# Taking the group statistics in a pass of their own and turning the image inside the layer norm

## The chip, the cores and the metric

One Trainium2 chip, one core. The metric is the device time of the kernel in microseconds (us): the median over runs of one build. Everything is fp32.

## The reference

The kernel computes four residual blocks on one image `x` of 256 x 256 pixels and 128 channels. Ahead of each block the image goes through a group norm with 32 groups of 4 channels. Only block 0 (attention over rows) and the layer norms of block 2 are touched. Cut to what matters:

```python
def _gn(v, G=32, eps=1e-5):                       # over the whole image, per group of channels
    g = v.reshape(B_, H_, W_, G, C_ // G)
    m = jnp.mean(g, axis=(1, 2, 4), keepdims=True)
    s = jnp.var(g, axis=(1, 2, 4), keepdims=True)
    return ((g - m) / jnp.sqrt(s + eps)).reshape(v.shape)

def _L0_conv_ref(z, ...):                         # z = _gn(x)
    mu = jnp.mean(z, axis=-1, keepdims=True)      # layer norm over the 128 channels of a pixel
    var = jnp.mean(jnp.square(z - mu), axis=-1, keepdims=True)
    zn = (z - mu) * jax.lax.rsqrt(var + EPS) * ln_scale + ln_bias
    q, k, v = zn @ Wq, zn @ Wk, zn @ Wv           # 4 heads of 32
    bias = zn @ Wb                                # one number per pixel and head
    ...

x = x + _L0_conv_ref(_gn(x), ...)                 # attention
x = x + _L1_conv_ref(_gn(x), ...)                 # recurrence in a transformed domain
x = x + _L2_conv_ref(_gn(x), ...)                 # triangle product, two layer norms
x = x + _L3_conv_ref(_gn(x), ...)                 # 3 x 3 convolution
```

## The kernel before

The input lies pixel by pixel, the kernel works channel by channel: 128 channels on 128 partitions, pixels along the free dimension. `run` goes through these stages one after the other; between stages the whole image (33.5 MB) goes out to HBM and comes back.

1. **Transposing stage** (`transpose_in`, L158 to L216). 64 blocks of 1024 pixels. SP loads a block of `x`, TensorE turns it in 8 transposes of 128 x 128 into the PSUM tile `pt`, VectorE (L208) and ScalarE (L206) each copy one half of it into `xo` in SBUF, VectorE takes `BATCH_NORM_STATS2` of `xo` (L211), and GpSimd issues the DMA that writes `xo` to the HBM image `xT` (L212). In between, `spectrum` makes the transforms of the recurrence's small kernels: TensorE products `ph`, ScalarE copies `H` (L188) and `HH` (L192), and a DMA to `HD`. `attention_weights` and `bounded` prepare block 0's weights on small tiles.
2. **Group norm's mean and variance** (`group_affine`, `centering`). A short chain on single columns; it yields `lc`, a 128 x 128 matrix that applies group norm and takes off the mean over channels in one product, and its constant `cb`.
3. **Layer norm stage of block 0** (first part of `attention`). For each block of 1024 pixels: product `zc` of `lc` with `xin`, loaded from `xT`; ScalarE squares `zc` to `sq`; VectorE adds `cb` and copies `zc` to `zs`; a product of `sq` with the full matrix `omat` gives the variance of each pixel on all 128 partitions at once (`var`, 128 x 1024); ScalarE takes its logarithm and exponential (`rs`); VectorE multiplies `zs` by `rs`; GpSimd applies scale and bias. For each 2048 pixels (a piece, in what follows) the products `pbias` with 32 weight columns follow, four side by side in one PSUM bank, the copy `bi`, four small DMAs to `biasD`, and a DMA of `zn` to the HBM image `znT`.
4. Attention itself (`attend_bounded`), then the recurrence.
5. **Triangle block** (`triangle`): its first layer norm (32 pieces), the triangle products, its last layer norm with gates (32 pieces).
6. The convolution.

The order of the work on each engine is written out in the program. What is wrapped in `pin` (`keep_in_program_order`) keeps its place; a scheduler may move the rest[...]. Pools with `bufs=n` rotate through n buffers, and a writer waits until the last reader of the old content is done. Where two engines read the same PSUM tile, the built program makes the second reader wait for the first.

The triangle's first layer norm already takes its variance with 32 weight columns (`tmean`), four products side by side in one bank, so that logarithm and exponential work on 128 x 512 and not on 128 x 1024; a second product, `pr`, spreads the result over the partitions:

```python
def variance(ps, work, sq):
    var = ps.tile([P, 512], F32, name="var", tag="r", bufs=2)
    for k in range(4):
        mm(var[32 * k:32 * k + 32], m32, sq[k // 2][:, (k % 2) * 512:(k % 2 + 1) * 512])
    rs = work.tile([P, 512], F32, name="rs")
    act(rs, var, AF.Ln, bias=self.eps)
    act(rs, rs, AF.Exp, scale=-0.5)
    return rs
```

Of the kernel before, what the change touches and what calls it, by code (L numbers as in the profile page):

```python
# [30 lines left out]
class Kernel:  # L31
# [43 lines left out]
    def group_affine(self, pool, psum, stats, group, tag, whole=False, shift=None):  # L75
# [20 lines left out]
        pm = psum.tile([P, 2], F32, name=f"pm{tag}", tag="gn")  # L96
        self.mm(pm[:, 0:1], group, mv[:, 0:1])
        mg = pool.tile([P, 1], F32, name=f"mg{tag}")
        nc.vector.tensor_copy(mg, pm[:, 0:1])
        d = pool.tile([P, 1], F32, name=f"gd{tag}")  # L100
        nc.vector.tensor_sub(d, mv[:, 0:1], mg)
        v = pool.tile([P, 1], F32, name=f"gv{tag}")
        nc.vector.scalar_tensor_tensor(v, d, d, mv[:, 1:2], ALU.mult, ALU.add)
        pv = psum.tile([P, 2], F32, name=f"pv{tag}", tag="gn")
        self.mm(pv[:, 0:1], group, v)
        sd = pool.tile([P, 1], F32, name=f"sd{tag}")
        self.chain("table", self.act(sd, pv[:, 0:1], AF.Sqrt, bias=self.eps))
        ab = pool.tile([P, 2], F32, name=f"ab{tag}")
        nc.vector.reciprocal(ab[:, 0:1], sd)
        nc.vector.scalar_tensor_tensor(ab[:, 1:2], mg, -1.0, ab[:, 0:1], ALU.mult, ALU.mult)  # L110
        if whole:
            return ab, mg, sd
        return ab
# [44 lines left out]
    def transpose_in(self, xT, HD_, stats):  # L158

        nc, tc, I = self.nc, self.tc, self.i
        x = I["x"].rearrange("b h w c -> (b h w) c")
        CG = HC // 4
        with ExitStack() as c:
            sp = c.enter_context(self.pool(name="sp", bufs=1))
            io = c.enter_context(self.pool(name="p0", bufs=5))
            ps = c.enter_context(self.pool(name="p0s", bufs=3, space=PSUM))
            tu = self.load(sp, I["c_rows"], "tu")
            HH = sp.tile([46, N, HC], F32, name="HH")  # L170
            H, ka = [], []
            for n, (re, im) in enumerate((("A_real", "A_imag"), ("B_real", "B_imag"))):
                kr, ki = (I["L1_conv_" + y].rearrange("c p q -> p c q") for y in (re, im))
                k = sp.tile([3 * KS, HC, 32], F32, name=f"ka{n}")
                nc.gpsimd.memset(k, 0.0)
                for p0, q0, src in ((0, 0, kr), (0, KS, ki), (KS, 0, ki), (2 * KS, KS, kr)):
                    nc.scalar.dma_start(k[p0:p0 + KS, :, q0:q0 + KS], src)
                ka.append(k)
                H.append(sp.tile([P, N, CG], F32, name=f"H{n}"))

            def spectrum(g):

                n, g0 = divmod(2 * g, CG)
                ph = ps.tile([P, 2, N], F32, name="ph", bufs=2)
                for j in range(2):
                    for k in range(4):
                        self.mm(ph[32 * k:32 * k + 32, j], ka[n][:, CG * k + g0 + j, :], tu)
                nc.scalar.copy(H[n][:, :, g0:g0 + 2].rearrange("q u c -> q c u"), ph)  # L188
                if g0 + 2 == CG:
                    o = slice(32 * n, 32 * n + 2 * KS)  # L190
                    for k in range(4):
                        nc.scalar.copy(HH[o, :, CG * k:CG * (k + 1)], H[n][32 * k:32 * k + 2 * KS])  # L192
                    nc.sync.dma_start(HD_[n], HH[o])

            NB = NPIX // 1024
            for b in range(NB):
                xin = io.tile([P, 8, P], F32, name="xin")
                nc.sync.dma_start(xin, x[b * 1024:(b + 1) * 1024].rearrange("(p t) c -> p t c", t=8))
                xo = io.tile([P, P, 8], F32, name="xo")
                pt = ps.tile([P, 8, P], F32, name="pt")  # L200
                for t in range(8):
                    nc.tensor.transpose(pt[:, t, :], xin[:, t, :], self.ident)
                for h in range(2):
                    o, i = xo[:, :, 4 * h:4 * h + 4], pt[:, 4 * h:4 * h + 4, :].rearrange("c t p -> c p t")
                    if h:
                        nc.scalar.copy(o, i)  # L206
                    else:
                        nc.vector.tensor_copy(o, i)  # L208
                xf = xo.rearrange("c p t -> c (p t)")
                for h in range(2):  # L210
                    nc.vector.bn_stats(stats[:, 2 * b + h, :], xf[:, h * 512:(h + 1) * 512])  # L211
                nc.gpsimd.dma_start(xT[:, b * 1024:(b + 1) * 1024], xf)  # L212
                if b == NB * 7 // 8 - 1:
                    self.early_statistics(stats, "0")
                if b >= 12 and b % 3 == 0 and b < 60:
                    spectrum(b // 3 - 4)  # L216

    def attention_weights(self, wp):

        nc, tc, I = self.nc, self.tc, self.i  # L220
        with self.pool(name="awp", bufs=1, space=PSUM) as ps0:
            def load(src, name):
                t = wp.tile(list(src.shape), F32, name=name)
                nc.scalar.dma_start(t, src)
                return t
            lns, lnb = (load(I["L0_conv_ln_" + n].rearrange("(c o) -> c o", o=1), "ln" + n[0]) for n in ("scale", "bias"))
            w, wb, raws = {}, {}, {}

            for nm, f in (("q", -1.0 / math.sqrt(HD)), ("k", 1.0), ("v", 1.0), ("g", 1.0), ("b", -1.0)):
                raw = raws[nm] = load(I["L0_conv_W" + nm], "raw" + nm)  # L230
                m = raw.shape[1]
                pb = ps0.tile([P, 2], F32, name="pb" + nm, tag="gn")
                self.mm(pb[:m, 0:1], raw, lnb)
                wb[nm] = wp.tile([m, 1], F32, name="wb" + nm)
                nc.vector.tensor_scalar_mul(wb[nm], pb[:m, 0:1], 0.5 if nm == "g" else f)
                w[nm] = wp.tile([P, m], F32, name="w" + nm)
                nc.vector.tensor_scalar(w[nm], raw, lns, f, ALU.mult, ALU.mult)
            wo = {"f": load(I["L0_conv_Wo"], "wo"), "h": wp.tile([P, P], F32, name="woh")}
            nc.vector.tensor_scalar_mul(wo["h"], wo["f"], 0.5)
            self.lnb = lnb  # L240
        small = self.bounded(wp, raws, w, wb)
# [7 lines left out]
        return w, (lns, lnb), wo, small  # L249
# [21 lines left out]
    def attention(self, wp, weights, later, xT, x1T, znT, biasD, stats0, stats1, shift1):  # L271
        nc, tc, I = self.nc, self.tc, self.i
        w, (lns, lnb), wo, small = weights
        with ExitStack() as c:
            with ExitStack() as c1:
                ps0 = c1.enter_context(self.pool(name="awq", bufs=2, space=PSUM))
                ab, mg, _ = self.group_affine(wp, ps0, stats0, self.g4, "0", True)
                nc.vector.tensor_scalar_mul(shift1, mg, -1.0)
                lc, cb = self.centering(wp, ps0, ab, "0")

            bias = wp.tile([P, 2, NH, N], F32, name="bias")
            first = tuple(wp.tile([P, 1024], F32, name=n) for n in ("zn0", "xr0"))

# [9 lines left out]
            with ExitStack() as c1:  # L293
                io = c1.enter_context(self.pool(name="a1", bufs=3))
                work = c1.enter_context(self.pool(name="a1w", bufs=3))
                ps = c1.enter_context(self.pool(name="a1s", bufs=2, space=PSUM))
                V = nc.vector
                wb32 = w["32"]
                pin = lambda f: lambda *a, **k: tc.keep_in_program_order(f(*a, **k))
                mm, act, tt, ts = pin(self.mm), pin(self.act), pin(V.tensor_tensor), pin(V.tensor_scalar_add)  # L300
                copy = pin(V.tensor_copy)
                flat = lambda t: t.rearrange("p k n -> p (k n)")
                NB = NPIX // 1024
                xin, zn, zc, zs, sq = {}, {}, {}, {}, {}

                def centre(b):
                    if b >= NB:
                        return
                    if b % 2 == 0:
                        xin[b // 2] = io.tile([P, 2048], F32, name="xin")  # L310
                        nc.sync.dma_start(xin[b // 2], xT[:, b * 1024:(b + 2) * 1024])
                        zn[b // 2] = io.tile([P, 2048], F32, name="zn")
                    zc[b] = ps.tile([P, 2, 512], F32, name="zc")
                    for k in range(2):
                        s = (b % 2) * 1024 + k * 512
# [22 lines left out]
                def pair_bias(m):  # L338
                    if m < 0:
                        return  # L340
# [1119 lines left out]
```

## Time and profile before

| what | value |
|---|---|
| median of 3 runs | 5201.29 us (5197.82 to 5203.03) |
| profiled execution | 5192.49 us, of which the span of the profile is 5190.7 us |
| busy share of the span | TensorE 95%, VectorE 79%, ScalarE 69%, GpSimd 8% |
| start to first transposes | 0 to 21 us |
| transposing stage | 21 to 221 us |
| group norm's mean and variance | 221 to 225.4 us |
| layer norm stage of block 0 | 225.4 to 491.9 us |
| first layer norm of the triangle | 3284 to 3519.5 us |
| last layer norm of the triangle | about 4220 to 4640 us |

The stage bounds are read off the timeline: the last copy `xo` begins at 218.3 us, the first `zc` at 225.4 us, the last copy `bi` ends at 491.9 us. In the page's rows a matrix product in fp32 appears as two instructions, so four products side by side are eight rows. The granted TensorE clock (PEclk) is a mean over a stretch of time, 1.00 being full.

### The profile page before, as it was taken

What the parts mean: (1) busy time and instruction counts of PE and PEld (TensorE: products, weight loads), DVE (VectorE), ACT (ScalarE), POOL (GpSimd) and SP (SyncE); (2) the same over time, 40 slices, a digit from 0 to 9 for tenths busy, and PEclk for the clock granted to TensorE, in tenths of its full rate; (3) what the DMA queues carried; (4) which work ended last, traced back from release to release, by engine and by line L of the source; (5) the groups of instructions that cost most, each with busy time, mean ns of one, the idle gap of its engine ahead of it and who ended that gap; (6) DMA issues with size and microseconds to landing.
All of it is one profiled execution on the core that took longest, in us unless ns stands there. A gap on an engine that the chain in (4) does not pass through costs nothing.

```text
span 5190.7 us, 77032 instructions
## 1 busy us (share of the span) xinstructions
PE 4917.5 (95%) x30579; PEld 2748.2 (53%) x30579; DVE 4111.6 (79%) x4888; ACT 3556.5 (69%) x4987; POOL 421.7 (8%) x616
## 2 busy tenths in 40 slices
PE   5699999999999899999999999789999989989999
PEld 4433555555555333333333333228999953339999
DVE  5666999999999799999999999665334427779886
ACT  4377888888888799999999999443333347762110
POOL 1232000000000000000000000240110010000000
PEclk7699999999999899999999999999999999999999
DMA  8875222222222222222222221677667768865432
GB/s 294 342 269 208 74 86 82 79 85 86 82 81 83 67 67 70 71 66 71 67 74 67 71 71 58 251 276 270 230 230 252 244 241 334 323 239 188 144 120 66
DMA packets 185926, 788.66 MB, mean 152 GB/s; under 512 B 36083, under 2 KB 39432, under 8 KB 136384
## 3 DMA queue, kind: packets, MB, share of 16 engines
q1 hardware_dynamic: 120212, 514.73, 29.6%
q0 software_dynamic: 60416, 268.46, 13.5%
q8 instruction: 244, 4.00, 0.3%
q10 hardware_dynamic: 4936, 0.50, 0.1%
q14 instruction: 118, 0.97, 0.1%
HBM read 512.28 MB, written 271.32 MB: 151 GB/s over the span
## 4 chain that ended last, share of the span: by engine, by line
PE 54%; DVE 29%; issue 12%; ACT 2%; POOL 1%; DMA 1%; POOLq 0%; ACTq 0%; SPq 0%; DVEq 0%
PE m L60 7%; PE zc L60 7%; PE nd L60 7%; PE sc L60 5%; PE z L60 4%; PE var L60 3%; DVE tr L806 3%; DVE t L803 3%; DVE y L803 3%; DVE p L803 3%; DVE yf L803 3%; PE ppq L60 3%; PE ppv L60 2%; PE px L60 2%; PE pe L60 2%
## 5 line engine op out<-in xcount | busy, mean ns | idle before, releaser
L471 DVE TENSOR_TENSOR e<-sc,bT 128x1024 f32<-128x1024 f32 x512 | 603.2, 1220 | 51.5 <-PE sc L60 51.5
L54 ACT ACTIVATE e<-e 128x1024 f32<-128x1024 f32 x512 | 540.2, 1055 | 63.2 <-DVE e L471 53.8
L966 DVE TENSOR_TENSOR LR<-z,sg 128x512 f32<-128x512 f32 x256 | 268.0, 1048 | 369.1 <-ACT sg L54 361.9
L60 PE MATMUL m<-U,v 128*128 128x128 f32 x4608 | 516.8, 276 | 6.6 <-DVE v L1307 6.6
L60 PEld LDWEIGHTS m<-U,v 128*128 128x128 f32 x4608 | 516.6, 193 | 6.7 <-DVE v L1307 6.7
L60 PE MATMUL z<-wf,zt 128*128 128x128 f32 x4096 | 461.7, 276 | 3.4 <-DVE LR L966 2.1
L60 PEld LDWEIGHTS z<-wf,zt 128*128 128x128 f32 x4096 | 461.3, 193 | 4.6 <-DVE LR L966 2.2
L54 ACT ACTIVATE sg<-z 128x512 f32<-128x512 f32 x256 | 152.8, 597 | 311.9 <-PE z L60 308.7
L471 DVE TENSOR_TENSOR ks<-e 128x1024 f32<-128x1024 f32 x256 | 300.9, 1217 | 0.0
L60 PE MATMUL sc<-tq,tk 32*128 32x256 f32 x4096 | 297.7, 402 | 3.2 <-DVE e L471 2.3
L60 PE MATMUL zc<-xin,lc 128*128 128x512 f32 x512 | 250.0, 612 | 44.2 <-DVE zs L966 43.6
L60 PEld LDWEIGHTS sc<-tq,tk 32*128 32x128 f32 x4096 | 186.9, 185 | 160.5 <-issue 97.1
L60 PE MATMUL nd<-e,tv 128*32 128x256 f32 x4096 | 271.8, 383 | 0.0
L54 ACT ACTIVATE dn<-dn 128x512 f32<-128x512 f32 x384 | 241.6, 629 | 12.6 <-DVE dn L471 1.9
L60 PE MATMUL av<-y,ident 128*128 128x512 f32 x384 | 192.2, 609 | 44.0 <-DVE y L803 44.0
L60 PE MATMUL po<-LR 128*128 128x256 f32 x1024 | 222.4, 380 | 8.1 <-DVE LR L966 7.0
L54 ACT ACTIVATE sq<-zc,cb 128x1024 f32<-128x1024 f32 x128 | 141.5, 1105 | 128.1 <-PE zc L60 128.1
L1344 ACT COPY m4s<-m 128x512 f32<-128x512 f32 x32 | 18.7, 584 | 287.6 <-PE m L60 287.5
L60 PEld LDWEIGHTS po<-LR 128*128 128x128 f32 x1024 | 194.1, 190 | 35.5 <-DVE LR L966 7.7
L60 PEld LDWEIGHTS zc<-xin,lc 128*128 128x128 f32 x512 | 93.5, 192 | 189.4 <-issue 94.4
L60 PE MATMUL bx<-p,ident 128*128 128x512 f32 x384 | 192.3, 610 | 0.0
L54 ACT ACTIVATE o<-po 128x256 f32<-128x256 f32 x256 | 84.2, 381 | 146.7 <-issue 115.9
(333 smaller groups left out, 10334.9 us busy)
## 6 DMA issues: line engine op xcount, KB each, us to landing
zt<-znT SPq DMA_DIRECT2D x128, 1024.0 KB
znT<-zn POOLq DMA_DIRECT2D x64, 1024.0 KB, 4.9
xin<-x2T SPq DMA_DIRECT2D x64, 1024.0 KB
xr<-x3T SPq DMA_DIRECT2D x46, 768.0 KB
xin<-in_x_dram SPq DMA_DIRECT2D x64, 512.0 KB
xT<-xo POOLq DMA_DIRECT2D x64, 512.0 KB, 10.6
xr<-xT SPq DMA_DIRECT2D x64, 512.0 KB
xin<-xT SPq DMA_DIRECT2D x32, 1024.0 KB
```

What stands on the lines that cost most here:

```text
L54: return self.nc.scalar.activation(out, in_, func, bias=bias, scale=scale, **kw)
L60: return self.nc.tensor.matmul(out, lhsT, rhs, start=start, stop=stop)
L471: pin = lambda f: lambda *a, **k: tc.keep_in_program_order(f(*a, **k))
L803: pin(V.tensor_tensor(out, a, b_, op))
L806: pin(V.scalar_tensor_tensor(out, a, k, b_, op0, op1))
L966: pin = lambda f: lambda *a, **k: tc.keep_in_program_order(f(*a, **k))
L1344: nc.scalar.copy(m4, m[4])
```

## The change

`transpose_in` goes. In its place stand a pass that only takes sums, and a layer norm stage that does the transposing itself.

- **Statistics** (`statistics`). All of `x` is loaded in 32 pieces of 1 MB. Pixels lie on the partitions here. VectorE subtracts the first pixel's channels (`sh`) from a half piece into `xs` (128 x 1024), ScalarE squares `xs` into `sqx`, and TensorE sums over the partitions with 32 columns of ones: the two halves of `xs` and the two halves of the preceding `sqx` stand side by side on the four 32-partition strips of one PSUM bank, `acc`, which collects over the whole image. At the end `acc` is copied and four small products with `sel` give mean and variance per channel. `x` is loaded in the order 6 to 31, then 0 to 5; the last six pieces stay in SBUF (`kept`, 48 KB per partition).
- **Layer norm stage** (`attention`). For each piece m: `turn` transposes (16 transposes into two tiles `pt`), ScalarE and then VectorE copy the halves into `xo`, GpSimd issues the DMA of `xo` to `xT`; `centre` takes `zc` straight from `xo`, VectorE copies it to `zs`, ScalarE squares `zs`; `variance` and the spreading product `pr` are those of the triangle block. Pieces 0 to 5 come from `kept`, the others are loaded from `x` a second time; `xT` is not loaded here.
- **Squares from the copies**. In both layer norms of the triangle, too, `zs` is copied out of PSUM first and `sq` is taken from `zs`, where before both were taken from `zc`.
- `kernel_rows` makes the transforms of the recurrence's kernels during the statistics. Its small loads are issued by GpSimd and no longer by ScalarE, and half of the `HH` copies go to GpSimd. The weights' loads and products stand apart (`next(weights)`).

In the order in which the built program issues them, 26 of the 64 squares, all 16 `H` copies and all 8 ScalarE `HH` copies stand ahead of the last 38 squares on ScalarE. In the layer norm stage the order for a piece is, on VectorE: `xo`, `xo`, `zs`, `zn`, `zn`, `bi`, `zs`; on ScalarE: `xo`, `xo`, `rs`, `rs`, `sq`, `sq`; on TensorE: `pt`, `pt`, `var`, `zc`, `pr`, `pbias`, `zc`. Every VectorE `xo` there carries a wait on ScalarE.

```diff
+    def statistics(self, wp, weights, HD_, kept, src):
...
+            def add_up(*pair):
                 for h in range(2):
...
+                    for j, t in enumerate(pair):
+                        if t is not None:
+                            o = 64 * j + 32 * h
+                            self.mm(acc[o:o + 32], ones[:, :32], t[:, h * 512:(h + 1) * 512],
+                                    start=count[j] < 2, stop=count[j] >= 4 * NM - 2)
+                            count[j] += 1
+
+            order = list(range(KEPT, NM)) + list(range(KEPT))
+            spectrum = None
+            for n, m in enumerate(order):
+                if m < KEPT:
+                    xin = kept[m]
+                else:
+                    xin = io.tile([P, 2, 1024], F32, name="xin", bufs=3)
+                nc.sync.dma_start(xin, src(m))
+                for b in range(2):
+                    xs = io.tile([P, 1024], F32, name="xs")
+                    V.tensor_tensor(xs.rearrange("p (t c) -> p t c", t=8), xin[:, b].rearrange("p (t c) -> p t c", t=8),
+                                    sh.unsqueeze(1).to_broadcast([P, 8, P]), ALU.subtract)
+                    sq = io.tile([P, 1024], F32, name="sqx")
+                    self.act(sq, xs, AF.Square)
+
+                    add_up(xs, last)
+                    last = sq
...
+            def turn(m):
+                if m >= NM:
+                    return
+                load(m + 2)
+                xo[m] = io.tile([P, 2, P, 8], F32, name="xo")
+                for b in range(2):
+                    pt = wide("pt").rearrange("c (t p) -> c t p", t=8)
+                    for t in range(8):
+                        transpose(pt[:, t], xin[m][:, b, t * P:(t + 1) * P], self.ident)
+                    for h, f in enumerate((acopy, copy)):
+                        f(xo[m][:, b, :, 4 * h:4 * h + 4], pt[:, 4 * h:4 * h + 4].rearrange("c t p -> c p t"))
+                nc.gpsimd.dma_start(xT[:, m * 2048:(m + 1) * 2048], xo[m].rearrange("c b p t -> c (b p t)"))
+
+            def centre(m, b):
+                if m >= NM:
+                    return
+                zc = wide("zc")
+                for k in range(2):
+                    mm(zc[:, k * 512:(k + 1) * 512], lc, xo[m][:, b].rearrange("c p t -> c (p t)")[:, k * 512:(k + 1) * 512])
+                zs[m, b] = work.tile([P, 1024], F32, name="zs")
+                ts(zs[m, b], zc, cb)
+                sq[m, b] = work.tile([P, 1024], F32, name="sq")
+                act(sq[m, b], zs[m, b], AF.Square)
...
+            turn(0)
+            centre(0, 0)
+            centre(0, 1)
+            for m in range(NM):
+                turn(m + 1)
+                variance(m)
+                centre(m + 1, 0)
+                normalise(m)
+                pair_bias(m - 1)
+                centre(m + 1, 1)
...
-                    sq[m, b] = work.tile([P, 1024], F32, name="sq")
-                    act(sq[m, b], zc, AF.Square, bias=cb)
                     zs[m, b] = work.tile([P, 1024], F32, name="zs")
                     add(zs[m, b], zc, cb)
+                    sq[m, b] = work.tile([P, 1024], F32, name="sq")
+                    act(sq[m, b], zs[m, b], AF.Square)
```

In the layer norm stage the PSUM tiles `pt`, `zc` and `pr` take turns in three buffers of two banks each (`wide`), `var` and `pbias` in two of one bank.

## The prediction

> **What bounds the kernel now.** The busy shares of the whole span (TensorE 95%) say little about the two stages that the change rewrites, so I read the table of busy time by stage first.
>
> ```profile
> core 0: us, PE busy (x) PEld busy (x) DVE busy (x) ACT busy (x) POOL busy (x), PEclk, DMA share, GB/s
> 21.00:221.00 200.00, 117.81 (x745) 91.95 (x743) 119.53 (x193) 78.56 (x87) 33.49 (x63) 0.67 0.95 351
> 221.00:225.40 4.40, 1.73 (x7) 1.54 (x7) 2.25 (x13) 1.54 (x2) 0.00 (x0) 0.50 0.53 216
> 225.40:491.90 266.50, 262.27 (x769) 100.89 (x770) 174.30 (x160) 204.55 (x193) 94.74 (x96) 0.99 0.66 247
> 3284.00:3519.50 235.50, 189.06 (x769) 58.51 (x768) 154.61 (x128) 111.20 (x129) 91.67 (x94) 1.00 0.76 286
> 4252.00:4600.00 348.00, 348.00 (x1075) 136.30 (x1073) 252.77 (x268) 257.16 (x268) 14.38 (x27) 1.00 0.89 333
> ```
>
> Row one, the transposing stage, is bound by DMA: share 0.95 at 351 GB/s, no engine over 60% busy. Row three, block 0's layer norm, is bound by TensorE (262 of 266.5 us), DMA at 0.66. Row four, the triangle's first layer norm, has nothing full. Row five, its last, is TensorE throughout (348 of 348). The waits between 40 and 220 us confirm row one:
>
> ```profile
> ACT xo L206 <- DVE xo L208: 92.2, 33, 10.1
> DVE xo L208 <- DMA xT<-xo: 48.2, 20, 10.5
> ```
>
> VectorE's copies wait for `xo` to be written out, and ScalarE's for VectorE's. For row four the timeline shows a whole turn of the loop:
>
> ```profile
> start us, us, engine line op out<-in xcount [idle before <-releaser]
> ...
> 3381.18 1.98 PE L60 MATMUL zc<-xin,lc 128*128 128x512 f32 x4 [1.46 <-DVE zs L966]
> ...
> 3383.20 1.11 ACT L54 ACTIVATE sq<-zc,cb 128x1024 f32<-128x1024 f32 x1 [3.40 <-PE zc L60]
> ...
> 3384.09 1.98 PE L60 MATMUL zc<-xin,lc 128*128 128x512 f32 x4
> ...
> 3386.11 1.11 ACT L54 ACTIVATE sq<-zc,cb 128x1024 f32<-128x1024 f32 x1 [0.54 <-PE zc L60]
> 3387.26 1.28 DVE L966 TENSOR_SCALAR zs<-zc,cb 128x1024 f32<-128x1024 f32 x1 [1.63 <-ACT sq L54]
> 3388.46 2.34 DVE L966 TENSOR_TENSOR zn<-zs,pr 128x1024 f32<-128x1024 f32 x2
> 3388.60 1.99 PE L60 MATMUL zc<-xin,lc 128*128 128x512 f32 x4 [1.45 <-DVE zs L966]
> ```
>
> From `zc` at 3381.18 to `zc` at 3388.60 is 7.42 us: zc 1.91, var 1.00, zc 2.02, sq 1.15, zs 1.34. It is a chain through three engines, none of them full: `zs` cannot read the PSUM tile before `sq` has.
>
> **What the Trainium skill says.** "PSUM — Partial Sum Buffer", Terms: two engines on one bank and quadrant collide, "reads against reads included". The trace agrees: there `zs` waited 85.3 us for `sq` in 64 instructions. "TensorE: Matmul & The Clock Gate", Part 3: products with 32 columns run side by side on the array's strips. It agrees: `var` with 32 columns takes 1.06 us for its eight rows, against 3.6 for eight rows of `omat`. Same page, Part 1 and Part 4: an idle stretch of about 3.4 us halves the clock, and transposes don't count as busy. The trace fits: clock 0.67 with the transposes, 1.00 in row four with TensorE 80% busy.
>
> **The change, part by part.**
>
> *Statistics replace the transposing stage.* Removed: 33.5 MB of writing, 128 BATCH_NORM_STATS2 (0.68 us each). Left per piece of 1 MB: at 351 to 367 GB/s (the latter from 4220 to 4240 us, loads alone) 2.9 us of DMA; VectorE 2 x 1.22; ScalarE 2 x 1.03; TensorE 2 x 1.06 at full clock. So DMA bounds, except where ScalarE also makes `H` and `HH`. Its queue ahead of the last 38 squares: 26 squares and 16 `H` at 1.03, and 8 half `HH` at 1.9 (half of 3.60 plus its fixed part), 58.5 us. The first subtraction comes at about 13 us (weights and the first loads as before), the first square at 14.5, and some 3 us go to a table load and waits: 76 us. SP's DMAs to `HD` wait in front of loads meanwhile; three buffers cover that. Of the 19 pieces then left four are loaded; 15 follow: 76 + 5 (a buffer to come free, latency) + 15 x 2.86 = 124 us. The last piece's VectorE, ScalarE, TensorE work and the copy of `acc` add 5.5: 129.5. Four `pmx` products and four small VectorE steps, 2.2, then the old chain from `pm` to `zc`, 3.5 (221.9 to 225.4): transposes start at 135, against `zc` at 225.4 before.
> Not shown: `acc` at half clock costs 2.1 us per half piece and bounds the last 19 pieces, +26; loads at 400 GB/s give -4; the kernels' small loads, now issued by GpSimd, took up to 11.7 us from ScalarE (19.25 to 30.93), and 6 us later than I assume (20 us) is +5. I take 129.5 and keep 125 to 155.
>
> *Layer norm stage.* Prices per piece from the rows above: 16 transposes 1.8 (8 took 1.09), zc 3.8, var 1.0, pr 1.1, pbias 1.0: TensorE 8.7. VectorE: xo 1.3, zs 2.4, zn 2.3, bi 0.6: 6.6. ScalarE: xo 1.2, sq 1.9, rs 1.35: 4.4. DMA: 3.15 MB at 351 GB/s, 9.0, and only 6.0 for the six kept pieces. None of these decides: the queues form a ring. `zs` of half 1 ends; `sq` 0.05 + 0.92 (start to start) holds ScalarE; its `xo` 0.59; then VectorE's `xo`, which reads the same tile, 0.05 + 0.68; `zc` of half 0 needs that `xo`, 0.06 + 1.98; `zs` 0.04 + 1.20; then VectorE's queue has zn, zn 2.27, bi 0.61, and `zs` of half 1 1.28. Sum **9.73 us** against 8.06 before (row three's loop: `var` at 301.70 and 309.76). 32 x 9.73 = 311, filling, draining and a cold clock at the start 12: the stage ends at 135 + 323 = 458 against 491.9. **Both stages together: -34.** So the transposes cost 57 of the 91 us that the statistics save. The second loading of `x` is hidden by the ring up to 0.93 of the DMA's rate; GpSimd's extra issues (0.5 us each, 32 fewer than before) lie beside 6 idle us per piece; `biasD` stands on SP ahead of loads that are needed two pieces later. The longer live buffers `kept` are read before anything else needs their space.
>
> *Squares from the copies, first layer norm of the triangle.* Now `zs` follows `zc` at once and frees it; the ring becomes zc 2.02, zs 1.33, sq 0.92, rs 0.72 and 0.63, pr 1.14: 6.8, and a little for queueing, 7.05. 31 x 0.37 = **-11**. Bounds: 0, if another wait takes over, to -19 at 6.8; TensorE needs 5.9, DMA 2.1 MB / 351 = 6.0.
> *Last layer norm.* Both readers are on ScalarE, TensorE is full: **0**. ScalarE, 74% busy, hides the wait of `sq` for `zs`; without that cover it would be about 0.25 us per piece, 8.
>
> Sum: -34 - 11 = -45 on the profiled execution's 5192.5, that is 5147.5. The median stands 8.8 above it: 5201.3 - 45 = **5156**.
>
> **Rivals.**
> - *The rings don't bind* (queues overlap better than I lay them out): TensorE's 8.7 bounds, -32 more: 5124. For it: row three ran at TensorE's pace. Against: every VectorE `xo` waits for ScalarE, and row four's ring did bind.
> - *A smaller gain*: mixed traffic falls to the 294 GB/s of the page's first slice, 10.7 us for 26 pieces, +25; or the statistics run cold, +26: 5182. For: loads and writes share the engines, and 3.15 MB per ring is 324 GB/s already. Against: 351 was held for 200 us, 356 at 3290 to 3350.
> - *Slower: the clock.* The new loop mixes transposes with waits. At the 0.67 of row one TensorE's 8.7 becomes 13.0, +3.3 x 31 = +101: 5257. It decides from a ring of 9.73 + 45/31 = 11.2 on, a granted clock under 0.78. For: row one. Against: that row had idle stretches of up to 11 us, the new ring's longest is below 2, and row four held 1.00 with stretches of 1.5.
> - *The triangle's part does nothing*: 5167, inside the first case.
>
> **How the numbers follow.** First case 0.62 (its own range 5138 to 5174: ring 9.4 to 10.1, triangle 0 to -19); rings don't bind 0.08; smaller gain 0.16; clock 0.14. A measurement of this kernel can tell about 0.2%, 10 us, from no change. Faster: 0.62 + 0.08 + 0.10 = 0.80; same: 0.05 + 0.02 = 0.07; slower: 0.01 + 0.12 = 0.13. Range 5126 to 5192: the first case, most of the second and third; the clock case is left out.
>
> **What would show it.** Transposes begin near 135 us and `bi` ends near 458; in between the loop turns in 9.7 us, with VectorE's `xo` waiting for ScalarE and TensorE idle before `zc` of half 0; ScalarE is full from 15 to 76 us, DMA from there on. The triangle's loop turns in 7.0 us, with no `zs` waiting for `sq`; the last layer norm keeps 13.0. Wrong would be: PEclk under 0.9 in either new stage, a ring set by DMA landings, or later stages that shift by more than 3 us.

## The result

The changed kernel takes 5186.68 us (median of 12 runs, 5174.85 to 5195.44) against 5200.46 us of the kernel before on the same chip (12 runs): ratio 0.9973, 95% interval 0.9965 to 0.9982. It is faster, as forecast, but by 14 us and not by 45; the time is 31 us above the predicted one. The profiled execution took 5189.01 us, with a span of 5187.2; it is only 3.5 us below the profiled one of before (5192.49), so the traces show a larger miss, 41.5 us, than the medians do.

The table of busy time by stage, kernel after; the columns are those of the table before:

```profile
23.40:83.00 59.60, 57.03 (x327) 11.69 (x327) 30.39 (x45) 34.16 (x33) 8.45 (x4) 0.63 0.52 173
83.00:110.00 27.00, 18.94 (x150) 4.78 (x146) 7.73 (x7) 24.20 (x21) 7.57 (x4) 0.81 0.70 208
110.00:170.00 60.00, 42.82 (x296) 6.69 (x298) 42.76 (x36) 39.30 (x38) 0.00 (x0) 0.89 0.81 283
...
176.50:498.20 321.70, 313.03 (x1537) 128.31 (x1538) 212.34 (x224) 142.04 (x193) 111.80 (x128) 0.98 0.84 304
3287.50:3517.00 229.50, 191.03 (x771) 59.05 (x770) 154.54 (x128) 107.62 (x129) 92.36 (x94) 1.00 0.79 295
4252.00:4600.00 348.00, 348.00 (x1071) 136.42 (x1071) 252.76 (x268) 266.31 (x270) 14.40 (x27) 1.00 0.89 333
```

The last three rows came as forecast, or nearly: layer norm stage 321.7 us (forecast 323), the triangle's first layer norm with a loop of 7.16 us instead of 7.42, its last layer norm unchanged. Between the two, attention and recurrence took 2.9 us less than before, which nothing in the change explains. The first three are the statistics. I had ScalarE full there from 15 to 76 us; instead ScalarE is busy for 34 of the first 59.6 us, TensorE for 57, and its clock is 0.63. The copy of `acc`, with which the sums end, was forecast to be done at 129.5 us, and is done at 171.5; the transposes begin at 176.5 and not at 135. In the profiled execution that is the whole miss. The line of the copy:

```profile
170.83 0.69 DVE L260 COPY accs<-acc 128x512 f32<-128x512 f32 x1 [2.30 <-PE acc L60]
```

In what follows "copy of `acc`" is its start, 170.8 us here. The expectations below have 168.6 in its place; that is the start of the last square, not of the copy.

The timeline of the layer norm stage, kernel after, one turn (columns: start, duration, engine and line, operation):

```profile
310.11 1.27 DVE L371 TENSOR_SCALAR zs<-zc,cb 128x1024 f32<-128x1024 f32 x1
...
311.41 1.06 ACT L54 ACTIVATE sq<-zs 128x1024 f32<-128x1024 f32 x1 [2.99 <-DVE zs L371]
...
312.38 1.05 ACT L371 COPY xo<-pt 128x512 f32<-128x512 f32 x2
312.98 1.29 DVE L371 COPY xo<-pt 128x512 f32<-128x512 f32 x2 [1.60 <-ACT xo L371]
...
313.72 1.98 PE L60 MATMUL zc<-xo,lc 128*128 128x512 f32 x4
...
315.75 1.28 DVE L371 TENSOR_SCALAR zs<-zc,cb 128x1024 f32<-128x1024 f32 x1 [1.48 <-PE zc L60]
...
319.81 1.27 DVE L371 TENSOR_SCALAR zs<-zc,cb 128x1024 f32<-128x1024 f32 x1
```

From `zs` at 310.11 to `zs` at 319.81 is 9.70 us (forecast 9.73), link by link as summed. The waits of the same stage name the two links that the change added, VectorE's `xo` behind ScalarE's, and `zc` behind VectorE's `xo`:

```profile
DVE xo L371 <- ACT xo L371: 53.2, 33, 2.7
...
PEld zc L60 <- DVE xo L371: 32.7, 31, 1.1
```

**Where the statistics lose time** shows in three places. First, the waits of the first 26 us:

```profile
DVE woh L301 <- DMA wo<-in_L_conv_Wo_dram: 5.2, 1, 5.2
...
DVE junk L494 <- DMA m<-in_c_block_dram: 4.1, 1, 4.1
```

Two steps of the weights' preparation wait on VectorE for loads. The first `xs` stands behind them in VectorE's queue until 23.36 us; no wait for its own load is recorded, and `sh` was written at 6.7 us. Second, the table in steps of 10 us:

```profile
30.00:40.00 10.00, 9.11 (x82) 2.24 (x82) 7.17 (x16) 8.95 (x10) 0.00 (x0) 0.92 0.70 230
40.00:50.00 10.00, 10.00 (x62) 2.43 (x58) 4.27 (x4) 4.70 (x6) 0.00 (x0) 0.50 0.53 194
50.00:60.00 10.00, 10.00 (x53) 1.75 (x56) 3.61 (x3) 5.31 (x6) 0.00 (x0) 0.50 0.56 184
60.00:70.00 10.00, 10.00 (x66) 2.45 (x62) 3.75 (x4) 3.96 (x5) 0.00 (x0) 0.50 0.40 131
70.00:80.00 10.00, 10.00 (x47) 1.39 (x43) 4.57 (x4) 6.73 (x5) 8.45 (x4) 0.50 0.31 105
```

TensorE is booked as full for 40 us, and its clock stays at half all the while. Twelve half pieces pass in that time, 6.7 us per piece. Third, the timeline around the second pair of writes to `HD`:

```profile
121.62 0.87 SPq L197 DMA_DIRECT2D HD<-HH  x2
...
137.96 2.36 DVE L244 TENSOR_TENSOR xs<-xin,sh 128x1024 f32<-128x1024 f32 x2 [8.68 <-DMA xin<-in_x_dram]
```

VectorE waits 8.7 us for the loads behind them; behind the first pair it had waited 7.0 us. In the trace's list of transfers each of the four writes consists of 14 packets of 32 KB, one per partition, with up to 14 under way at once. One takes 1.2 to 5.1 us, where a 4 KB packet of the loads takes 0.16, and the two pairs fill 84.1 to 93.5 us and 125.6 to 133.9 us.

### The profile page after: what moved, and what is told of

Read it like the earlier page. It is cut to its first block, busy times and chain, and to the rows that moved or that the text cites. A ratio compares the mean times of both kernels' runs of the same rounds, so it can differ in the third digit from the quotient of the medians.

```text
span 5187.2 us, 78333 instructions
## 1 busy us (share of the span) xinstructions
PE 4965.6 (96%) x31357; PEld 2702.8 (52%) x31357; DVE 4108.0 (79%) x4829; ACT 3518.2 (68%) x4988; POOL 427.6 (8%) x600
## 4 chain that ended last, share of the span: by engine, by line
PE 53%; DVE 29%; issue 5%; ACT 2%; POOL 0%; DMA 0%; SPq 0%; POOLq 0%; DVEq 0%; ACTq 0%
PE z L60 9%; PE m L60 7%; PE nd L60 7%; PE sc L60 5%; PE po L60 4%; DVE tr L896 3%; DVE t L893 3%; DVE y L893 3%; DVE p L893 3%; DVE yf L893 3%; PE ppq L60 3%; PE ppv L60 2%; PE zc L60 2%; PE px L60 2%; PE pe L60 2%
## 5 line engine op out<-in xcount | busy, mean ns | idle before, releaser
L54 ACT ACTIVATE sq<-zs 128x1024 f32<-128x1024 f32 x192 | 203.0, 1057 | 284.5 <-DVE zs L371 157.7
L60 PEld LDWEIGHTS nd<-e,tv 128*32 128x32 f32 x4096 | 120.2, 110 | 109.8 <-issue 44.2
```

Of the source, the lines that this page charges most:

```text
L54: return self.nc.scalar.activation(out, in_, func, bias=bias, scale=scale, **kw)
L60: return self.nc.tensor.matmul(out, lhsT, rhs, start=start, stop=stop)
```

## The experiments

My theory was that these are three separate causes, each to be taken away alone. The rivals were that the clock would be low anyway, that the writes and small loads are only neighbours of loads that are slow by themselves, and that one cause hides another.

**Products padded to 128 rows.** The spectrum's products contract over 21 rows.

```diff
-        tu = self.load(sp, I["c_rows"], "tu")
+        tu = sp.tile([P, N], F32, name="tu")
+        nc.gpsimd.memset(tu, 1.0)
+        nc.sync.dma_start(tu[:3 * KS], I["c_rows"])
...
-            k = sp.tile([3 * KS, HC, 32], F32, name=f"ka{n}")
+            k = sp.tile([P, HC, 32], F32, name=f"ka{n}")
```

> The changed kernel, but the spectrum's products `ph` contract over 128 rows instead of 21: the kernels' tile is padded with zeros, `tu` with ones, so results and the time of one product at a given clock stay as they are. In the changed kernel TensorE is booked as full from 40 to 80 us, yet its clock stays at 0.50. Theory A: the 21-row products, which fill a sixth of the array's rows, don't count as activity for the clock, and keep it at half. Then PEclk is 1.00 (over 0.9) from 40 to 80 us here, a piece takes what ScalarE needs (two squares, one `H`, half an `HH` pair: 4.0 us) instead of 6.6, and the last copy of `acc` comes about 15 us earlier, near 153 instead of 168.6; the run takes 5170 to 5177 against 5187. Theory B: the clock stays low for another reason (short waits between the groups of products, or the 32-column form itself): PEclk stays 0.50 there, and the time is within 4 us of the changed kernel's.

5169.63 us (5169.18 to 5172.34), ratio 0.9943 (0.9927 to 0.9960). The table of this run:

```profile
30.00:60.00 30.00, 25.73 (x263) 10.14 (x255) 19.33 (x15) 25.76 (x26) 7.50 (x4) 1.00 0.78 262
```

Clock 1.00, and now ScalarE is the fuller engine; the copy of `acc` began at 150.1. That fits theory A. But the first `xs` started at 18.5 us here, 4.9 earlier than in the changed kernel's profile; a later run shows that the start varies by more than that from one execution to the next. So some of the 17 us is not the padding's.

**Small loads behind the weights.**

```diff
             nc.gpsimd.memset(k, 0.0)
+            nc.gpsimd.tensor_scalar(k[:3 * KS, 0, :], self.m32[:3 * KS, :32], 0.0, None, ALU.mult)
```

(and `next(weights)` ahead of `kernel_rows`, so that `m32` is known there.)

> The changed kernel, but GpSimd issues the small loads of the convolution kernels only after the last weight (`m32`) has landed (a small GpSimd operation on that tile stands ahead of them). In the changed kernel VectorE's queue stood 5.2 us for `wo` and 4.1 us for `m32`, with the first subtraction `xs` behind them at 23.4 us. Theory A: the kernels' small pieces, issued from 4.2 us on, filled the DMA engines ahead of the weights. Then `m32` lands near 11 us, the first `xs` starts at 13 to 14, and everything up to the copy of `acc` comes 7 to 10 us earlier: 5177 to 5180. Theory B: the weights' own loads and the first megabytes of x are what takes the time; then `xs` starts at 21 to 24 as before and the time doesn't change. Theory C: the start is earlier, but the spectrum's products wait for the late kernels, and TensorE's queue with them: `xs` at 13 but the copy of `acc` at 165 or later.

5170.79 us (5168.41 to 5174.15), ratio 0.9943 (0.9926 to 0.9959). The timeline of this run:

```profile
10.52 0.57 POOL L177 TENSOR_SCALAR ka<-m 21x32 f32<-21x32 f32 x2 [6.23 <-DMA m<-in_c_block_dram]
...
13.59 2.35 DVE L245 TENSOR_TENSOR xs<-xin,sh 128x1024 f32<-128x1024 f32 x2
```

`m` is there at 10.5 us, `xs` starts at 13.59: theory A. The copy of `acc` came at 151.8, 19 us earlier and not 10: the clock, too, was low for a shorter time in this profile (0.86 over 30 to 40, 1.00 over 40 to 60). VectorE still waited 17.8 us for `xin`. In all five runs with the small loads late the first `xs` starts at 13.5 to 13.8 us; where they are early, it starts anywhere from 16.2 to 23.5.

**Writes to `HD` behind the last load.**

```diff
-                    nc.sync.dma_start(HD_[n][:, u], HH[o])
+                    self.held.append((HD_[n][:, u], HH[o]))
...
+            for o, i in self.held:
+                self.tc.add_manual_dep(nc.sync.dma_start(o, i).ins, ld.ins.name, NOSYNC, reason="last load")
```

> The changed kernel, but the four writes of the spectra to `HD` (448 KB each, from 14 partitions) are issued behind the last load of the statistics. In the changed kernel VectorE waited 7.0 us (to 98.1) and 8.7 us (to 138.0) for a load after each pair of writes. Theory A: the writes hold the loads up by more than their bytes[...]: without them in between both stalls vanish, and since the second lies in the stretch that DMA sets, the copy of `acc` comes 8 to 12 us earlier; part may come back as a wait of the layer norm's first tiles for the space that the writes read. Time 5175 to 5181. Theory B: the stalls are the loads' own rate; moved writes give nothing, copy of `acc` at 167 to 169, time within 4 us of the changed kernel's.

5173.22 us (5169.31 to 5176.64), ratio 0.9947 (0.9930 to 0.9964), copy of `acc` at 150.5. VectorE's waits for loads shrank from 16.7 us to 1.5. Yet the clock was back at 1.00 by 50 us in this profile, so the 20 us in the trace (170.8 to 150.5) are not the writes' alone. Up to 50 us this kernel issues the same work as the changed one, and its first `xs` came as late (23.5 us): the late start by itself does not settle how long the clock stays at half.

**No spectrum at all.** The products `ph` and the copies `H` and `HH` are left out.

> The changed kernel without the work on the convolution kernels' spectra in the statistics: the products `ph`, the copies `H` and `HH` are left out, the tile `HH` is zeroed and written to `HD` at the end, so the output is not the reference's. What is left is the statistics alone. If my sum was right in its other terms, the stage is bound by DMA: the clock is at 1.00 from 40 us on, and 32 pieces of 2.86 us from the first `xs` at 23.4 on end at 115 to 120 us, 50 us earlier than in the changed kernel: 5135 to 5142. If `acc`'s 32-column products alone keep the clock at half (2.1 us per half piece, 4.2 per piece), the stage ends at 155 to 160, 5175 to 5180. If loads alone run at 400 GB/s, 110 us.

5136.56 us (5132.27 to 5140.14), ratio 0.9881 (0.9864 to 0.9897). From the first `xs` at 16.2 to the copy of `acc` at 114.0 it takes 97.8 us, 3.06 per piece, with the DMA engines at a share of 0.98 and the clock at 0.95: the statistics alone are bound by loads, as I had said (at 2.86 per piece), and everything above that comes from the spectrum beside them, 43 to 50 us by the medians of the changed kernel's two sets of runs.

**The changed kernel once more.**

> The changed kernel unaltered, once more, for the clock. In its first profile TensorE stayed at half clock for 45 us in the statistics, in the variant with late writes, with the same instructions up to there, for about 10 us. Theory A: whether and when the clock comes back within the spectrum's products is chance[...]; then this profile shows half clock for another length of time (10 to 60 us between 30 and 110 us), the last copy of `acc` comes between 145 and 175 us, and the runs spread over 15 us or more. Theory B: it is the same each time: half clock from 38 to 83 us, copy of `acc` at 167 to 170, and the spread of the runs comes from elsewhere.

5179.34 us (5173.78 to 5186.75; 5 runs), ratio 0.9965 (0.9952 to 0.9979). Theory A, though the runs spread over 13.0 us and not 15: in this profile (5173.78 us) the first `xs` came at 16.4 us, the clock was 0.67 over 30 to 40 us and 0.99 over 40 to 50, and the copy of `acc` came at 154.0. The same program thus starts its first `xs` 7 us earlier or later. Two profiles with the late start (this kernel's first and that of the swapped copies below) have the clock at half for 40 us, but the run with late writes, which started as late, for about 10. What decides it stays open. Over the first 12 runs the time goes with the granted clock of the run: 5188.6 to 5195.4 us at 0.982, 5174.9 at 0.987.

**Do rows count?** The statistics without spectrum, with 21 of 128 rows:

```diff
-                            self.mm(acc[o:o + 32], ones[:, :32], t[:, h * 512:(h + 1) * 512],
+                            self.mm(acc[o:o + 32], ones[:21, :32], t[:21, h * 512:(h + 1) * 512],
```

> The statistics without the spectrum, as in the run above, and `acc` sums only over the first 21 of the 128 partitions, so the statistics are of a sixth of the data and the output is not the reference's. Instructions, columns and transfers are those of the run without the spectrum, where PEclk was 0.97 over 20 to 110 us. Theory A: the clock's activity counts the rows of the array in use. Then products of 21 rows, though they keep TensorE as busy, leave the clock at 0.50 through the whole statistics; a half piece takes 2.1 us of TensorE instead of 1.2, 64 of them 134 us, and the copy of `acc` moves from 114.0 to 145 to 155 us: 30 to 40 us more than the 5136.6 of the run without the spectrum. Theory B: rows don't matter: PEclk above 0.9, copy of `acc` at 113 to 116, 5133 to 5140.

5152.84 us (5152.65 to 5153.88), 16 us more than with 128 rows; copy of `acc` at 133.6 instead of 114.0. The timelines, this run's first, then the same stretch with 128 rows:

```profile
60.81 1.06 PE L60 MATMUL acc<-xs,ones 21*32 21x512 f32 x1
...
61.66 1.06 PE L60 MATMUL acc<-xs,ones 21*32 21x512 f32 x1
```

```profile
61.86 0.62 PE L60 MATMUL acc<-xs,ones 128*32 128x512 f32 x1 [1.27 <-DVE xs L237]
...
62.31 0.59 PE L60 MATMUL acc<-xs,ones 128*32 128x512 f32 x1
```

Rounds of four products start 0.85 us apart with 21 rows, all through the stage, and 0.45 with 128. That is the pace of the half clock (1.06 us per product and 0.85 between rounds in the changed kernel from 40 us on). 21-row products aren't slow as such: `ph` has a median of 374 ns in the runs where the clock was up, against 379 padded. And the eight `pmx` products right behind the stream, which use all 128 rows in both runs, have a median of 353 ns here and 251 there: what was slow is TensorE, not the shape of the products. So the durations speak for theory A, while PEclk reads 1.00 throughout this one profile. My size was too high: a half piece took 1.7 us, not 2.1. The clock without the spectrum, which the expectation gives as 0.97 over 20 to 110 us, is 0.94 in the table of that stretch. The Trainium skill, "TensorE: Matmul & The Clock Gate", Part 1, warns that the clock's events in a trace can be unreliable; here spacing and durations decide.

**Two of three, and all three.** First padding and late small loads together:

> The changed kernel with two of the three edits, the spectrum's products padded to 128 rows and the kernels' small loads behind the weights; the writes to `HD` stay where they are. Between the run with the late kernel loads alone (copy of `acc` at 151.8 us, 5170.8) and that with all three (132.0, 5156.6) it tells the clock from the writes. Theory A, both matter: the clock is at 1.00 through 30 to 60 us, ScalarE's part ends near 85 us instead of 91, VectorE still waits for a load after each pair of writes, and the copy of `acc` comes at 140 to 147: 5162 to 5168. Theory B, the writes are all of the difference: 5169 to 5172. Theory C, the clock is all of it: 5155 to 5159.

5167.31 us (5163.66 to 5167.48), ratio 0.9939 (0.9923 to 0.9956), nearest to theory A: the copy of `acc` came at 148.7, a little later than I said, and VectorE waited 9.9 us for `xin` after 60 us. But the clock over 30 to 60 us was 0.95 and not 1.00, the same as without the padding (0.95 with late small loads alone); only over 60 to 100 us was it higher, 0.83 against 0.70. Then late small loads and late writes, unpadded:

> The changed kernel with the kernels' small loads behind the weights and the writes to `HD` behind the last load, but the spectrum's products at 21 rows as they were. It tells what the padding is worth when the other two causes are gone (all three together: copy of `acc` at 132.0 us, 5156.6, runs within 4 us of each other). Theory A, the 21-row products keep costing clock: PEclk under 0.9 over 30 to 50 us in the profile as in the run with the late kernel loads alone, copy of `acc` at 134 to 142, 5159 to 5166, and a spread of the runs of 6 us or more. Theory B, with an early start the clock costs nothing: 5153 to 5158, and the padding is only worth something where the start is late.

5164.77 us (5155.90 to 5169.67; 5 runs), ratio 0.9933 (0.9920 to 0.9947), copy of `acc` at 137.9. Theory A, though the clock was low later than I said (0.98 over 30 to 60 us, 0.63 over 80 to 90). Then all three:

> The changed kernel with the three edits together: the spectrum's products padded to 128 rows, the kernels' small loads behind the weights, the writes to `HD` behind the last load. Theory A, the three are separate causes and the stage is otherwise as I summed it: first `xs` at 13.5 us, clock 1.00 from 30 us on, no wait of VectorE for a load after 110, copy of `acc` at 128 to 138 us; the run takes 5150 to 5160. Theory B, they cover for one another, so that two of them give nothing beside the first: copy of `acc` at 147 to 152, 5168 to 5173.

5156.61 us (5152.96 to 5156.79), ratio 0.9917 (0.9902 to 0.9932). This is theory A: the copy of `acc` came at 132.0. The clock is 1.00 over 30 to 60 us, though it dips to 0.66 over 60 to 70. The table of this run, from the first `xs` to the copy of `acc`:

```profile
13.70:132.00 118.30, 97.65 (x771) 26.30 (x771) 88.79 (x88) 96.58 (x90) 24.49 (x15) 0.96 0.83 270
```

The medians make a ladder: changed kernel 5186.7 and 5179.3, late small loads 5170.8, with padding 5167.3, with late writes 5156.6. The last step is clear in the runs (none of the four below 5163 without it, none above 5157 with it), the one before it lies within the intervals. (In these rounds the median of the kernel before moved between 5197.5 and 5200.5, so a step of 3 us can't be told.) From the other side the padding takes 8 us off (5164.8 to 5156.6; the intervals overlap) and the spread of the runs from 13.8 us (5 runs) to 3.8 (4 runs). In the traces the padding can be told from the start, since both runs of each pair start their first `xs` within 0.1 us of each other: the copy of `acc` comes 3.0 us earlier (151.8 to 148.7) and 6.0 us earlier (137.9 to 132.0), and the mean clock over 30 to 100 us goes from 0.81 to 0.88 and from 0.87 to 0.94. Each edit alone gives 6 to 17 us, all three some 23 to 30: to some extent they overlap. An earlier start that also shortens the spell at half clock would explain part of it; that is not shown.

**The triangle's part alone**, on the kernel before:

```diff
-                    sq[m, b] = work.tile([P, 1024], F32, name="sq")
-                    act(sq[m, b], zc, AF.Square, bias=cb)
                     zs[m, b] = work.tile([P, 1024], F32, name="zs")
                     add(zs[m, b], zc, cb)
+                    sq[m, b] = work.tile([P, 1024], F32, name="sq")
+                    act(sq[m, b], zs[m, b], AF.Square)
```

> The kernel before with one part of the change alone: in the triangle's first layer norm the squares are taken from the copy `zs` instead of from the PSUM tile `zc`. In the changed kernel that loop turned in 7.16 us instead of 7.42. Theory A: the part is worth 31 x 0.26 = 8 us wherever it stands: ratio 0.9984 to the kernel before, 5191. Theory B (my sum): 11 us, ratio 0.9979. Theory C: what comes after gives it back (ratio 0.9995 or more).

5190.90 us (21 runs) against 5198.97 (25 runs), ratio 0.9985 (0.9978 to 0.9992): 8 us, nearest to theory A, though my 11 lies inside the interval too.

**The order of the two copies in the layer norm ring.**

```diff
-                    for h, f in enumerate((acopy, copy)):
+                    for h, f in ((1, copy), (0, acopy)):
```

> The changed kernel, but VectorE copies its half of each transposed tile `pt` to `xo` first and ScalarE the other half second, in the layer norm of block 0. If the ring is what I summed (9.70 us measured), VectorE's copy (0.68) then lies beside ScalarE's square (0.92), and the ring loses 0.65 to 0.7: 9.0 us, the stage is 20 us shorter and the run 20 us faster than the changed kernel's 5179 to 5187, near 5163. Rival 1, DMA: 3.15 MB in 9.0 us is 349 GB/s, and waits for `xin` or for `xo` to be written out take over: ring 9.3 to 9.7, gain 0 to 10 us. Rival 2, VectorE: its copy now waits for the transposes ahead of other work in its queue, and the ring doesn't change.

5175.12 us (5168.28 to 5185.80), ratio 0.9952 (0.9935 to 0.9969). The 20 us did not come. The ring lies in the range that I gave for the first rival, but not for its reason: no wait for `xin` or for `xo` to be written out shows in this stage. The timeline of this run:

```profile
309.25 1.28 DVE L371 COPY xo<-pt 128x512 f32<-128x512 f32 x2
309.36 1.06 ACT L54 ACTIVATE sq<-zs 128x1024 f32<-128x1024 f32 x1 [2.99 <-DVE zs L371]
309.55 1.97 PE L60 MATMUL var<-sq,mean 128*32 128x512 f32 x8
...
310.32 1.05 ACT L371 COPY xo<-pt 128x512 f32<-128x512 f32 x2
...
311.45 1.13 PE L60 MATMUL zc<-xo,lc 128*128 128x512 f32 x2
```

VectorE's copy does lie beside the square now, but the ring, `zc` at 301.91 to 311.45, is still 9.54 us. Two paths still lead from the square to `zc`: ScalarE's two copies, which now stand behind it and end at 311.37, and `var`, which stands ahead of `zc` on TensorE's queue, needs the same square with its second half and ends at 311.52. Both end within 0.1 us of the start of `zc`. The profile puts the wait down to ScalarE's copies (24.3 us in 29 turns); but the copy that `zc` of half 0 reads is the first of the two, done near 310.9, which speaks for `var`. This run doesn't settle it. The stage takes 6.5 us less (315.2 against 321.7; 31 turns of 0.16 make 5), not 20. All four edits together:

> All four edits on the changed kernel: the three in the statistics (5156.6 us together) and the order of the two copies. If they add, 5156.6 - 20 = 5136, ratio 0.988 to the kernel before; if the shorter ring runs into the DMA's rate, 5146 to 5156.

5152.99 us (5151.49 to 5155.64), ratio 0.9916 (0.9899 to 0.9932): the fastest version that computes everything, though the intervals don't tell it from the 5156.6 without the swap. It lies in my second range, but again not because of the DMA's rate: in the trace the layer norm stage is 6.3 us shorter than in that run (318.1 against 324.4), as with the swap alone.

## Why the prediction was right and wrong

- **Layer norm stage: right**, in size and mechanism. What I missed is that a second ring, by way of `var` or of ScalarE's copies, lies only 0.16 us below the first. The slower rival, TensorE's clock in this loop, did not come (0.98).
- **Triangle's first layer norm: right in sign, 8 us and not 11.** The loop turns in 7.16 us (forecast 7.05), along another ring than the one I summed. Its timeline in the kernel after:

```profile
3409.47 1.14 PE L60 MATMUL pr<-rs,tspread 32*128 32x512 f32 x8 [1.20 <-ACT rs L54]
...
3410.70 2.35 DVE L1056 TENSOR_TENSOR zn<-zs,pr 128x1024 f32<-128x1024 f32 x2 [1.04 <-PE pr L60]
...
3412.97 1.28 DVE L1056 TENSOR_SCALAR zs<-zc,cb 128x1024 f32<-128x1024 f32 x1
...
3414.28 1.06 ACT L54 ACTIVATE sq<-zs 128x1024 f32<-128x1024 f32 x1 [3.54 <-DVE zs L1056]
...
3416.63 1.14 PE L60 MATMUL pr<-rs,tspread 32*128 32x512 f32 x8 [1.19 <-ACT rs L54]
```

  The two `zn` on VectorE (2.27) stand ahead of `zs`, in the place where I had `zc` (2.02), and `pr` to `zn` is 1.23 rather than 1.14. No `zs` waits for `sq` any more. Their wait of before was one that the built program orders; no run here lets the two engines read the tile at once.
- **Last layer norm: right**, no change.
- **Statistics: wrong, by 42 us in the profiled execution** (copy of `acc` done at 171.5 against 129.5). This is the term that failed, in three steps. "The first subtraction comes at about 13 us (weights and the first loads as before)": the loads were not as before, since GpSimd issued the kernels' small loads from 4.2 us on. The first `xs` came at 23.4 and 16.4 us in two profiles, and at 13.6 with the small loads late. I had priced their coming late, not their coming early. "ScalarE's queue ... 76 us": I never priced TensorE in that stretch and took ScalarE for the bound. The spectrum's products were missing from the step, and at half clock they and `acc` take 6.7 us per piece where ScalarE needs about 4. The cold bound of +26 us was in the list, but for the last 19 pieces, where the clock was 0.89. "SP's DMAs to `HD` ...; three buffers cover that": they don't; VectorE waited 16.7 us for loads, 1.5 with the writes late.
- With the three taken away the copy of `acc` is done at 132.6, 3.1 us from the forecast, and the median is 5156.6, where I had said 5156. That the medians agree so well is in part luck: by the profiled executions this version is 35.8 us below the kernel before, where my sum said 45.
- So it was the rival "a smaller gain" with its cold statistics that came nearest in time (5182), though for another stretch of the stage than it named. That 5186.7 lies inside my whole range is owed to the width that the rivals gave it.

## What to carry to other kernels

When work is slid under another stage, add up every engine in that stretch, TensorE too, and ask what the new queue's first loads stand in front of. Thin products, few rows deep, may leave TensorE at half clock however full it looks; here padding them with zeros cost no more than 5 ns of 374 per product and went with a higher clock. Before a ring is shortened at one link, look for the second ring through the same instructions.

## What the runs showed of the hardware

- A TensorE that is booked as busy does not by itself bring the clock back: 40 us at 10.00 of 10 us busy with a clock of 0.50, in two profiles (this kernel's and that of the swapped copies), and 110 us of half-rate products with 21 rows alone. It isn't a fixed rule either: the same mix of 21 and 128 rows ran at 0.99 to 1.00 over 40 to 60 us in three other profiles (the changed kernel once more, late small loads, and these with late writes). With 128 rows throughout the clock over 30 to 60 us was 1.00 in three padded runs and 0.95 in the fourth, and 0.93 over 60 to 110 us for the sums alone, with waits for loads. The Trainium skill, "TensorE: Matmul & The Clock Gate", Part 1, gives about 3.4 us of sustained work for the return to full clock; the 40 us and the 110 us don't agree with it.
- Four writes of 448 KB, each from 14 partitions, cost the loads around them more than their 1.8 MB, which would be 5 us at 351 GB/s: 10.7 us by the medians (5167.3 to 5156.6), 16.7 in the traces (148.7 to 132.0). It isn't that only few transfers are under way at once: the trace has up to 14 packets of 32 KB together. At 1.2 to 5.1 us each the two pairs take 9.4 and 8.3 us. Why a packet takes so long when 14 are under way, no run here shows.
